# A loop over passes of two rounds, hand-written semaphores, and three larger pieces in two places

## The chip, the core and the metric

The kernel runs on one core of one Trainium2 chip. Four parts of the core matter here: VectorE (DVE in the profile), ScalarE (ACT), SyncE (SP), which issues the transfers, and the 16 DMA engines that move bytes between the on-chip buffer (SBUF, 128 partitions) and the chip's memory. The metric is the device time of one execution in microseconds, the median of several runs.

## The reference

For each of 4,096 rows of 256 numbers, all products of two numbers of the row are computed, and the upper triangle (with the diagonal) is kept: 256 x 257 / 2 = 32,896 float32 numbers per row.

```python
dot = jnp.einsum('bi,bj->bij', inputs, inputs)     # inputs: (4096, 256) float32
iu, ju = jnp.triu_indices(d)                       # d = 256
return dot[:, iu, ju]                              # (4096, 32896) float32
```

The input is 4.19 MB, the output 538.97 MB. In the output, a row is a sequence of runs: run i holds x[i] * x[i:], 256 - i numbers long.

## The kernel before

A partition holds 32 input rows. They are worked off in 16 groups of two rows (`REPEAT`). Of each group, the 32,896 output columns are cut into five pieces; each piece is computed for both rows into one of three buffers of a pool and stored with one DMA per row. The very first piece is cut further, so that stores can start early.

```python
UNIT = 64
REPEAT = 2
PIECES = 5
BUDGET = 0.95
FIRST = [512, 1536, 3584]
...
opool = ctx.enter_context(tc.tile_pool(name="o", bufs=3))
x_out = out.rearrange("(p g r) c -> g p r c", p=P, r=REPEAT)
...
cuts = [0, REPEAT * d, total // 2, total]
for a, b in zip(cuts, cuts[1:]):
    nc.sync.dma_start(xt[:, a:b], x_in[:, a:b])

for g in range(groups):
    for c, (lo, hi) in enumerate(zip(borders, borders[1:])):
        o = opool.tile([P, REPEAT, slot], F32, tag="o", name=f"o_{g}_{c}")
        first = g == c == 0
        cuts = [lo, *(FIRST if first else []), hi]
        for a, b in zip(cuts, cuts[1:]):
            block = runs(d, a, b)
            k = split(block, 0.0 if first else BUDGET * REPEAT * (b - a))
            for i, j, at, length in block[:k]:              # ScalarE: one run, one row
                for r in range(REPEAT):
                    nc.scalar.activation(o[:, r, ...], xt[...], AF.Copy, scale=xt[...])
            for (i, j, at, length), m in interleave(block[k:]):   # VectorE: one or two runs, both rows
                nc.vector.tensor_tensor(o[:, :, ...], window(xt...), window(xt...), ALU.mult)
            for r in range(REPEAT):
                nc.sync.dma_start(x_out[g][:, r, a:b], o[:, r, a - lo : b - lo])
```

`split` gives runs to ScalarE until what is left for VectorE fits in a budget (in ns, per column and row), or until ScalarE would take longer than VectorE. Its account of the two engines is in the kernel:

```python
def vector_time(block):
    return sum(68 + 1.046 * REPEAT * n * m for (*_, n), m in vector_ops(block))
...
scalar += REPEAT * (184 + 0.837 * block[k][3])
```

The 16 groups are unrolled in Python: the program has each group's instructions in full. The framework places the semaphores.

## Time and profile before

| What | Value |
|---|---|
| time, median of 3 runs | 1274.3 us (1274.18 to 1274.4) |
| span of the profiled execution | 1272.5 us |
| multiplications on VectorE | 1812, mean 634 ns |
| idle time of VectorE ahead of them | 239.9 us, of which 191.1 ended by a store that landed |
| runs on ScalarE | 1546, mean 404 ns |
| read from memory, written to it | 4.19 MB, 538.97 MB |

The page counts the busy time of each engine, shows the span in 40 slices (a digit is the busy share in tenths), the DMA queues with packets and bytes, and the chain of work that ended last. A packet is one contiguous stretch that one DMA engine moves. The times "to landing" run from the issue of a DMA on SyncE until its semaphore has been raised by all 16 engines, so they hold the time in line behind earlier DMAs too. Tables of stretches give, for each stretch of time, each engine's busy time with the number of instructions, and the mean share of the 16 DMA engines that was busy.

### The profile page before, as it was taken

To read this page: it belongs to the slowest core of one execution; us is meant where nothing else is said; L and a number is where in the kernel's file an instruction comes from. 1 tells how busy PE (TensorE), PEld (TensorE's weight loads), DVE (VectorE), ACT (ScalarE), POOL (GpSimd) and SP (SyncE) were. 2 spreads that over 40 slices of the span, in tenths; PEclk is the share of its full clock that TensorE was granted. 3 is DMA by queue.
4 is the path that set the end of the run, shared out by engine and by line. 5 is a ranking of instruction groups with operands and counts; after the bars stand their busy time and mean duration, and the time that the engine had idled before them with its cause. 6 is when DMAs were issued, how large, how long until landed. Compare 5 with 4: busy or idle time off the path is not lost.

```text
span 1272.5 us, 3975 instructions
## 1 busy us (share of the span) xinstructions
DVE 996.1 (78%) x1813; ACT 486.7 (38%) x1547; POOL 0.2 (0%) x4
## 2 busy tenths in 40 slices
DVE  8987887878777787777877777777777777777770
ACT  5523535234342433424334252342523425234250
POOL 0000000000000000000000000000000000000000
DMA  9999999999999999999999999999999999999998
GB/s 384 435 433 430 434 433 427 434 432 427 431 428 432 429 430 431 429 431 429 433 427 431 429 431 429 431 430 430 429 432 427 433 427 432 428 432 429 431 427 346
DMA packets 24367, 543.43 MB, mean 427 GB/s; under 512 B 2704, under 2 KB 2704, under 8 KB 3344
## 3 DMA queue, kind: packets, MB, share of 16 engines
q1 hardware_dynamic: 24336, 543.17, 99.8%
q14 instruction: 31, 0.25, 0.0%
HBM read 4.19 MB, written 538.97 MB: 427 GB/s over the span
## 4 chain that ended last, share of the span: by engine, by line
DMA 70%; DVE 25%; issue 1%; SPq 1%; DVEq 0%
DMA out_dram<-o 70%; DVE o L132 25%; SPq L139 1%; DMA x<-in_r_inputs_dram 1%; DVEq L132 0%; SPq L110 0%
## 5 line engine op out<-in xcount | busy, mean ns | idle before, releaser
L132 DVE TENSOR_TENSOR o<-x 128x356 f32<-128x356 f32 (+61 forms) x1812 | 996.1, 634 | 239.9 <-DMA out_dram<-o 191.1
L123 ACT ACTIVATE o<-x 128x253 f32<-128x253 f32 (+41 forms) x1546 | 485.4, 404 | 748.6 <-DMA out_dram<-o 732.8
L123 ACT ACT_TABLE_LOAD x1 | 1.3, 1283 | 0.7 <-PEq L154 0.7
L107 DVE MEMSET x<- 128x1 f32 x1 | 0.1, 59 | 0.8 <-PEq L154 0.8
L154 POOL MEMSET const-uint8-127<- 128x1 uint8 x1 | 0.1, 102 | 0.0
L154 POOL MEMSET const-bfloat16-1.0<- 128x1 bf16 x1 | 0.1, 101 | 0.0
L154 POOL MEMSET const-float32-0.0<- 128x1 f32 x1 | 0.1, 98 | 0.2 <-issue 0.2
L154 POOL MEMSET const-float32-1.0<- 128x1 f32 x1 | 0.1, 98 | 0.0
## 6 DMA issues: line engine op xcount, KB each, us to landing
out_dram<-o SPq DMA_DIRECT2D x128, 3296.0 KB, 27.2
out_dram<-o SPq DMA_DIRECT2D x30, 3264.0 KB, 28.9
out_dram<-o SPq DMA_DIRECT2D x2, 1472.0 KB, 13.3
x<-in_r_inputs_dram SPq DMA_DIRECT2D x1, 2048.0 KB, 12.3
out_dram<-o SPq DMA_DIRECT2D x2, 1024.0 KB, 10.0
x<-in_r_inputs_dram SPq DMA_DIRECT2D x1, 1792.0 KB, 6.8
out_dram<-o SPq DMA_DIRECT2D x2, 512.0 KB, 10.2
out_dram<-o SPq DMA_DIRECT2D x2, 256.0 KB, 10.0
```

Source lines behind the costliest of these rows:

```text
L107: nc.vector.memset(xt[:, total:], 0.0)
L123: nc.scalar.activation(o[:, r, at - lo : at - lo + length], xt[:, row + j : row + j + length], AF.Copy, scale=xt[:, row + i : row + i + 1],)
L132: nc.vector.tensor_tensor(o[:, :, at : at + m * length], window(xt[:, row + j :], [[d, REPEAT], [1, m], [1, length]]), window(xt[:, row + ...
L139: nc.sync.dma_start(x_out[g][:, r, a:b], o[:, r, a - lo : b - lo])
L154: nc = _bacc.Bacc("TRN2", target_bir_lowering=False, num_devices=1)
```

## The change

The same products are computed and stored, in another frame:

- Three pieces per group instead of five (44 KB per row instead of 26), so each place holds 2 x 44 KB. There are two such places instead of three buffers. The borders are multiples of 32 columns instead of 64.
- One DMA stores both rows of a piece.
- The 16 groups ("rounds") are taken two at a time: a pass has two rounds. The first pass is written out, the other seven are a loop on VectorE, ScalarE and SyncE[...]. The purpose is a program that is short and whose loop body stays where it is.
- [...] in each round VectorE and ScalarE each copy the group's two rows to buffers of their own (`xv`, `xa`), and read from these.
- Semaphores are written by hand. A wait that is passed takes its amount back from the semaphore, so that the next pass finds it at zero. VectorE counts its own instructions, and each waits until all but the one before it are done.
- The budget for VectorE is 0.9 instead of 0.95 ns.

The core of the diff (cuts marked with ...):

```diff
-UNIT = 64
+UNIT = 32
 REPEAT = 2
-PIECES = 5
-BUDGET = 0.95
+PIECES = 3
+PLACES = 2
+ROUNDS = 2
+BUDGET = 0.9
 FIRST = [512, 1536, 3584]
...
+    def take(self, engine, value: int):
+        engine.wait_ge(self.sem, value).then_inc(self.sem, -value)
...
-    opool = ctx.enter_context(tc.tile_pool(name="o", bufs=3))
+    xt = pool.tile([P, groups // ROUNDS, ROUNDS * each], F32, name="x")
+    xv = pool.tile([P, each + 1], F32, name="xv")
+    xa = pool.tile([P, each], F32, name="xa")
+    places = [pool.tile([P, REPEAT, slot], F32, name=f"o{k}") for k in range(PLACES)]
...
+        def add(self, ins, back: int = 1):
+            if self.count > back:
+                ins._wait_ge(v_own, self.count - back)
+            ins.then_inc(v_own, 1)
+            self.count += 1
...
+    def rounds(h, first: bool):
+        work = VectorWork()
+        for p in range(ROUNDS * PIECES):
+            r, c = divmod(p, PIECES)
+            k = p % PLACES
+            lo, hi = spans[c]
+            start = first and p == 0
+            if c == 0:
...
+                work.add(nc.vector.tensor_copy(xv[:, :each], x_now))
+                work.end()
+                nc.scalar.activation(xa, x_now, AF.Copy).then_inc(a_own, 1)
+                nc.scalar.wait_ge(a_own, 1).then_inc(a_own, -1)
+            if not (first and p < PLACES):
+                free[k].take(nc.vector, 16 * stores[k])
+                nc.vector.sem_inc(go.sem, 1)
+                go.take(nc.scalar, 1)
+            cuts = [lo, *(FIRST if start else []), hi]
             for a, b in zip(cuts, cuts[1:]):
                 block = runs(d, a, b)
...
+                vector_part(work, places[k], lo, block[share:])
+                work.end()
+                nc.vector.sem_inc(v_done.sem, 1)
+                if share:
+                    scalar_part(places[k], lo, block[:share])
+                    nc.scalar.wait_ge(a_own, 1).then_inc(a_own, -1)
+                nc.scalar.sem_inc(a_done.sem, 1)
+                v_done.take(nc.sync, 1)
+                a_done.take(nc.sync, 1)
+                nc.sync.dma_start(
+                    x_out[bass.ds(h, 1), r, :, :, a:b].rearrange("o p r c -> p (o r) c"),
+                    places[k][:, :, a - lo : b - lo],
+                ).then_inc(free[k].sem, 16)
...
+    rounds(0, first=True)
+    with nc.Fori(
+        1,
+        groups // ROUNDS,
+        1,
+        engines=ENGINES,
+        head_slot={mybir.EngineType.DVE: 0, mybir.EngineType.Activation: 0},
+    ) as h:
+        rounds(h, first=False)
```

## The prediction

> **What bounds the kernel now.** I read the slices and the queues of the page first, then the chain of waits, then the groups, then single stretches. The page:

> ```profile
> span 1272.5 us, 3975 instructions
> DVE 996.1 (78%) x1813; ACT 486.7 (38%) x1547; POOL 0.2 (0%) x4
> DMA  9999999999999999999999999999999999999998
> GB/s 384 435 433 430 434 433 427 434 432 427 431 428 432 429 430 431 429 431 429 433 427 431 429 431 429 431 430 430 429 432 427 433 427 432 428 432 429 431 427 346
> DMA packets 24367, 543.43 MB, mean 427 GB/s; under 512 B 2704, under 2 KB 2704, under 8 KB 3344
> q1 hardware_dynamic: 24336, 543.17, 99.8%
> q14 instruction: 31, 0.25, 0.0%
> DMA 70%; DVE 25%; issue 1%; SPq 1%; DVEq 0%
> out_dram<-o SPq DMA_DIRECT2D x128, 3296.0 KB, 27.2
> ```

> The DMA engines are full in every slice but the ends, near 430 GB/s, and VectorE is idle for 22% of the span. So the bytes bound it; the 25% of VectorE in the chain of waits only says that a free buffer is followed by 12.4 us of work. A store lands 27.2 us after issue though its own bytes take 3.375 MB / 430 GB/s = 7.85 us: over three stores stand in line, and that backlog hides VectorE. The timeline shows the same from its side:

> ```profile
> 92.68 12.42 DVE L132 TENSOR_TENSOR o<-x 128x768 f32<-128x768 f32 x17 [3.25 <-DMA out_dram<-o]
> 1208.32 12.38 DVE L132 TENSOR_TENSOR o<-x 128x612 f32<-128x612 f32 x21 [3.07 <-issue]
> 1224.10 12.74 DVE L132 TENSOR_TENSOR o<-x 128x372 f32<-128x372 f32 x48 [3.40 <-DMA out_dram<-o]
> ```

> A piece is 12.4 to 12.7 us of multiplying and then 3 to 4 us of waiting. Last, the table of stretches at both ends (us, DVE, ACT, POOL busy, PEclk, DMA share, GB/s):

> ```profile
> 0.00:10.00 10.00, 6.32 (x12) 7.88 (x19) 0.20 (x4) 1.00 0.84 336
> 10.00:20.00 10.00, 10.00 (x13) 9.19 (x27) 0.00 (x0) 1.00 0.99 370
> ...
> 1265.00:1266.00 1.00, 0.00 (x0) 0.00 (x0) 0.00 (x0) 1.00 0.50 211
> 1266.00:1267.00 1.00, 0.00 (x0) 0.00 (x0) 0.00 (x0) 1.00 0.19 79
> 1267.00:1269.00 2.00, 0.00 (x0) 0.00 (x0) 0.00 (x0) 1.00 0.18 79
> 1269.00:1270.00 1.00, 0.00 (x0) 0.00 (x0) 0.00 (x0) 1.00 0.12 53
> 1270.00:1271.00 1.00, 0.00 (x0) 0.00 (x0) 0.00 (x0) 1.00 0.06 26
> ```

> A share of 0.19 is 3 of 16 engines, 0.12 two, 0.06 one. Thirteen engines are done soon after 1266 and three stragglers run on to about 1271, the last some 5 us behind. The time is that of the slowest DMA engine.

> [...] The trace agrees: its packet records have medians of 84 ns for 2,048 B, 159 for 4,096, 309 for 8,192 and 980 for 26,368, which is about 9 ns plus 0.0368 ns per byte. [...] The trace has 31 instruction packets of 8 KB (309 ns each), so the fetches do share the DMA engines; that they sit on the three stragglers is my inference. [...]

> **The change part by part.**

> (a) Fewer packets. A store is 128 partitions x 2 rows, one packet each. Before: 80 pieces x 256 = 20,480, three extra cuts in the first piece x 256 = 768, loads 384: 21,632. After: 48 x 256 = 12,288, plus 768, plus 384: 13,440. That is 8,192 fewer. The 4-byte packets at a DMA's end fall from 169 x 16 to 54 x 16, 1,840 fewer. Per engine (8,192 + 1,840) / 16 = 627 packets x 9 ns = 5.6 us less. The bytes stay. All of it lies on the path. [...]

> (b) Fewer instruction fetches. By the built programs, VectorE goes from 1,894 instructions in the body[...] to 244 ahead of the loop and 242 in it; ScalarE from 1,705 to 242 and 223. [...] some 4 packets per engine. If one straggler carries VectorE's 15, it loses 11 x 309 ns = 3.4 us. I take 3.5[...].

> (c) The loop and its steps. Each round adds a copy of 512 elements on VectorE and one on ScalarE (by the neighbours in the groups, 0.5 to 0.7 us each), each piece a few semaphore steps (50 ns each on VectorE by the median of its semaphore instructions), each pass a branch. They stand where VectorE waits for a free place: off the path while slack is left.

> (d) Is there slack with two places? A store moves 2 x 43.9 KB x 128 = 11.24 MB, 26.1 us at 430 GB/s. A place comes free when its store has landed, and that is when the other store starts. Then: VectorE's part by the kernel's own account 19.5 to 19.7 us (the same account gives 12.26 to 12.44 for the old pieces, and the timeline 12.38 to 12.74, so I take 19.9); the start and landing of a DMA, 2.1 us (the first load, 256 KB, lands 2.7 us after issue, and its bytes take 0.6); semaphore hops and addresses, about 1. Sum 23.0, slack 3.1 us in each 26.1. ScalarE's largest part is 16.0 us and hides behind VectorE's. So the queue stays full, with 3 us instead of a backlog of nearly 20. Cost 0.

> (e) The start, where slack isn't yet built up. The first piece is cut at the same three columns, but its last part is now 7,360 columns instead of 2,944. VectorE's share of the four parts is 1.2 + 1.8 + 3.0 + 9.9 = 16.0 us. From 3.4, where the first load has landed, with 1.0 for the copy and a later entry and 0.8 for the four hand-overs, it is done at 21.2; the store flows at 22.4. The DMAs have 4.19 MB of loads and 3.67 MB of stores until then; by the table they moved 7.06 MB in 20 us, so they run dry near 22: no gap worth counting. The fourth part, 7.54 MB, lasts 17.5 us, to 40. The second piece needs VectorE from 21.3 to 41.2 and flows at 42.5. Gap 2.5 us, paid once.

> (f) Entry and exit of the hand-written part: a barrier at each end and the waits at the end, +0.8 us.

> Sum: -5.6 + 0.3 - 3.5 + 2.5 + 0.8 = -5.5. 1274.3 - 5.5 = 1268.8 us.

> **The rivals.**

> Two places starve the queue. If the hand-over costs 4 us more than I think (own-count waits on each multiplication, the branch, a slow address), slack turns into a gap of 1 us in each of 46 periods: 1320 us. For it: 3.1 us is thin, and the engines differ by 3 to 5 us in when they end. Against it: the program before has such a wait on nearly every multiplication too, and its pieces take what the kernel's account says, and an engine that runs ahead only waits for the slowest, which keeps its work in line.

> The loop fetches its body again in each pass. The line that ends in "issue" shows VectorE held up for about 3 us, and there are 15 of these; at each back edge it would fall into the 6 us in which VectorE waits anyway. The packets would stay as many as they were: (b) falls away, 1272.

> The bytes alone count. [...] (a) is worth 2 and the start eats the rest: 1273.

> VectorE as the bound: 16 x (19.5 + 19.7 + 19.7) = 942 us is far below the span. I discard it.

> **Range and chances.** The known terms go from -13[...] to +2 (no packet gain, a start gap of 4). Within them, 1264 to 1275 should hold 8 times in 10. Faster by over 2% needs 25 us[...]. Chance 0.01. Slower by over 2% needs the first rival in every period: 0.04. Within 2%: 0.95.

> **What would show it.** (a): about 14,300 packets and 432 GB/s in middle slices. (b): instruction packets near 10, and stragglers that end within 2 us of the rest. (c), (d): waits of VectorE for a store of 4 to 7 us in each period, and no slice in the middle below 9. (e): a DMA share below 1 for 2 to 3 us near 40 us. A dip in every period, or some 30 instruction packets, would prove me wrong in (d) or (b).

## The result, and the profile after

The changed kernel takes 1275.49 us (median of 4 runs, 1275.45 to 1275.53) against 1274.25 us before: a ratio of 1.001, with a 95% interval of 0.9992 to 1.0027. The prediction was 1268.8 us, with a range of 1264 to 1275.

The first part of the page of the changed kernel, its slices and queues:

```profile
span 1273.5 us, 4059 instructions
DVE 952.5 (75%) x1748; ACT 535.1 (42%) x1601; POOL 0.2 (0%) x4
DMA  9999999999999999999999999999999999999997
DMA packets 14315, 543.26 MB, mean 427 GB/s; under 512 B 864, under 2 KB 864, under 8 KB 1504
q1 hardware_dynamic: 14304, 543.17, 99.2%
q14 instruction: 11, 0.09, 0.0%
```

The packets fell from 24,367 to 14,315 and the instruction packets from 31 to 11, as predicted. The DMA engines are still full, and the rate over the whole span is 427 GB/s as before. In the middle it is hardly higher, first before, then after:

```profile
100.00:1200.00 1100.00, 873.45 (x1583) 421.76 (x1344) 0.00 (x0) 1.00 1.00 430
100.00:1200.00 1100.00, 837.90 (x1529) 463.73 (x1393) 0.00 (x0) 1.00 1.00 431
```

So the packets were saved, and the time that they had cost went elsewhere. The two ends show a part of it. Stretches of the changed kernel (us, DVE, ACT, POOL busy, PEclk, DMA share, GB/s; a packet is credited to the stretch in which it begins, and one lasts 1.6 us, so single shares are coarse):

```profile
38.00:40.00 2.00, 2.00 (x4) 0.00 (x0) 0.00 (x0) 1.00 0.55 236
40.00:42.00 2.00, 1.65 (x5) 0.73 (x3) 0.00 (x0) 1.00 0.21 88
42.00:44.00 2.00, 2.00 (x6) 2.00 (x8) 0.00 (x0) 1.00 1.41 597
1264.00:1266.00 2.00, 0.00 (x0) 0.00 (x0) 0.00 (x0) 1.00 0.81 351
1266.00:1268.00 2.00, 0.00 (x0) 0.00 (x0) 0.00 (x0) 1.00 0.06 22
1268.00:1270.00 2.00, 0.00 (x0) 0.00 (x0) 0.00 (x0) 1.00 0.10 44
1270.00:1272.00 2.00, 0.00 (x0) 0.00 (x0) 0.00 (x0) 1.00 0.00 0
```

Near 40 us the DMAs are dry: the packet records have nothing from 40.1 to 42.0. At the end one engine is left over: from 1268 on a share of 0.10 over 2 us is two packets of 1.62 us, one after the other on one engine. The trace also records each raise of a store's semaphore (a "mark" below; it doesn't say of which engine). Fifteen of the 16 engines mark the last store as done between 1267.36 and 1267.52, the sixteenth at 1271.79. The kernel waits for all 16 marks of a store (`free[k].take(nc.vector, 16 * stores[k])`, and `free[k].take(nc.sync, 16)` at the end), and the span ends 1.7 us after the last of them. So the sixteenth mark costs 4.3 us here.

In between VectorE has time to spare. The timeline of the changed kernel (start, length, instructions; in brackets the idle time before):

```profile
1193.76 19.70 DVE L158 TENSOR_TENSOR o<-xv 128x788 f32<-128x788 f32 x26 [6.54 <-DVEq L93]
1219.70 20.03 DVE L158 TENSOR_TENSOR o<-xv 128x484 f32<-128x484 f32 x62 [6.25 <-DVEq L93]
```

Where it waited 3 us for a buffer before, it waits 6 us for a place in each period of 26 us. From the last mark of a store at 1219.48 to the issue of the next store into the same place it is 20.6 us (issued at 1240.10), and the first packets begin 0.9 us later, at 1240.99. The late engine ends the store before at 1245.85, so it has 4.9 us to spare. The other 15 ended it near 1240.8 and stood still for some 0.2 us. From 770 us on the last mark stays 4.4 to 4.8 us behind the median of the 16: the slack is used up, and the others are held to the late engine's pace, since a place is free only when it, too, is done. Two places are enough for the engine that sets the time.

### The profile page after: what moved, and what is told of

The parts are those of the page before. It is cut to its first block, busy times and chain, and to the rows that moved or that the text cites. A ratio compares the mean times of both kernels' runs of the same rounds, so it can differ in the third digit from the quotient of the medians.

```text
span 1273.5 us, 4059 instructions
## 1 busy us (share of the span) xinstructions
DVE 952.5 (75%) x1748; ACT 535.1 (42%) x1601; POOL 0.2 (0%) x4
## 2 busy tenths in 40 slices
DMA packets 14315, 543.26 MB, mean 427 GB/s; under 512 B 864, under 2 KB 864, under 8 KB 1504
## 3 DMA queue, kind: packets, MB, share of 16 engines
q1 hardware_dynamic: 14304, 543.17, 99.2%
HBM read 4.19 MB, written 538.97 MB: 427 GB/s over the span
## 5 line engine op out<-in xcount | busy, mean ns | idle before, releaser
L158 DVE TENSOR_TENSOR o<-xv 128x672 f32<-128x672 f32 (+27 forms) x1731 | 945.6, 632 | 269.0 <-DVEq L93 268.4
L170 ACT ACTIVATE o<-xa 128x253 f32<-128x253 f32 (+49 forms) x1584 | 523.8, 423 | 686.5 <-ACTq L93 685.7
L193 DVE COPY xv<-x 128x512 f32 (+1 forms) x16 | 6.8, 427 | 17.3 <-issue 8.2
L195 ACT ACTIVATE xa<-x 128x512 f32 (+1 forms) x16 | 10.1, 630 | 13.4 <-issue 6.1
## 6 DMA issues: line engine op xcount, KB each, us to landing
out_dram<-o SPq DMA_DIRECT2D x1, 2048.0 KB, 12.4
```

What stands on the lines that cost most here:

```text
L158: nc.vector.tensor_tensor(o[:, :, at : at + m * length], window(xv[:, j:], [[d, REPEAT], [1, m], [1, length]]), window(xv[:, i:], [[d, REP ...
L170: ins = nc.scalar.activation(o[:, r, at - lo : at - lo + length], xa[:, r * d + j : r * d + j + length], AF.Copy, scale=xa[:, r * d + i : ...
L193: work.add(nc.vector.tensor_copy(xv[:, :each], x_now))
L195: nc.scalar.activation(xa, x_now, AF.Copy).then_inc(a_own, 1)
```

## The experiments

The order is that of the question: is it the fetches, the start, the engine itself, the bytes or the instructions? A ratio is against the kernel before, whose medians beside the experiments are 1274.20 to 1274.28 us.

**The loop written out** (e1).

```diff
-    with nc.Fori(1, groups // ROUNDS, 1, engines=ENGINES, head_slot=...) as h:
+    for h in range(1, groups // ROUNDS):
         rounds(h, first=False)
```

Expected:

> The changed kernel with its eight passes written out instead of looped; all else stays. Theory A (instruction fetches make the DMA engines that end last): about 30 instruction packets come back, one engine ends some 3 us later, and the time is 1278 to 1279 us. Rival B (the engine that ends last is slow for another reason, such as what it does to the stores themselves): the packets come back too, the time stays within 1 us of 1275.5.

Measured: 1275.08 us, ratio 1.0007 (0.9999 to 1.0015). Its queue row and its tail:

```profile
q14 instruction: 30, 0.25, 0.0%
```

```profile
1266.00:1268.00 2.00, 0.00 (x0) 0.00 (x0) 0.00 (x0) 1.00 0.16 66
1268.00:1270.00 2.00, 0.00 (x0) 0.00 (x0) 0.00 (x0) 1.00 0.15 66
1270.00:1272.00 2.00, 0.00 (x0) 0.00 (x0) 0.00 (x0) 1.00 0.05 22
```

The fetches came back, 30 instead of 11, and the time did not rise. There are more late engines (the last three marks are 1.3, 4.1 and 4.5 us behind the median), but the last is hardly later: 4.5 us for 4.4. What is gained lies behind it: from the last mark to the end of the span it is 1.2 us, with the loop 1.7. Theory A falls, and with it the reason for the loop: it saves nothing that can be seen.

Fetches can still have cost something on the way. In the changed kernel eight of the 11 instruction packets fall between 126 and 234 us (309 to 400 ns each, 2.6 us in all), and meanwhile the last mark goes from 0.7 to 3.4 us behind the median. After that none falls until the work is over, and the marks show two engines: one falls back, to 1.6 us at 667 us; another rises, from 1.6 us at 302 us to 4.5 at 770 us, while some 650 multiplications and 590 ScalarE instructions run. The delay that lasts grows without fetches.

**The second piece's first store cut in two** (e2).

```diff
+SECOND = [13696]
-            cuts = [lo, *(FIRST if start else []), hi]
+            cuts = [lo, *(FIRST if start else SECOND if first and p == 1 else []), hi]
```

> The changed kernel with the store of the second piece of the first pass cut in two (2,752 and 8,224 columns), so that the DMAs have work when the first piece's last part is done. Theory A (the dry stretch of 1.9 us near 40 us is a loss that is never given back): no dry stretch, 1273.5 us. Rival B (the time is set by how fast places come free later on, and the start is made up there): 1275.5 us.

Measured: 1273.54 us, ratio 0.9995 (0.9987 to 1.0003). The same stretches as above:

```profile
38.00:40.00 2.00, 2.00 (x4) 0.00 (x0) 0.00 (x0) 1.00 0.77 327
40.00:42.00 2.00, 1.24 (x4) 0.65 (x3) 0.00 (x0) 1.00 0.96 407
42.00:44.00 2.00, 2.00 (x5) 2.00 (x7) 0.00 (x0) 1.00 0.94 391
```

The share at 40 us goes from 0.21 to 0.96 and the time falls by 1.95 us, the length of the gap (1.87 us). Here the dry start is paid in full.

**Stores alone, in both shapes** (e3, e4). All computing is left out; zeros are stored.

```diff
-    (products, and waits between the engines)
+    for k in range(PLACES):
+        nc.vector.memset(places[k], 0.0).then_inc(filled, 1)
...
+            if n_store >= PLACES:
+                free[k].take(nc.sync, 16 * 1)
+            nc.sync.dma_start(x_out[...], places[k][...]).then_inc(free[k].sem, 16)
```

> Stores alone: no products are computed, two places of zeros are stored over and over with the changed kernel's shape, 48 DMAs of 2 x 44 KB per partition, two in line; the loads stay. Per packet overhead of 5 ns (the pitch of the last engine's packets): the stores take 1253 us of DMA time on each engine, 3 us less than in the next run. Overhead of 9 ns, as predicted: 5.6 us less. If instruction fetches make the stragglers, all 16 engines end within 1 us here; if one engine is slow by itself, it ends 3 to 5 us after the rest.

> Stores alone in the shape of the kernel before: 160 DMAs of one row of 26 KB per partition, three places of two DMAs in line; no products are computed. 3 us longer than the run with the 44 KB shape if a packet costs 5 ns, 5.6 us if 9 ns, under 1 us if the packet's size doesn't matter. Stragglers as in that run.

Measured: 1300.05 us with 44 KB, 1301.38 us with 26 KB. The fills ahead of the first store differ, so I count from its issue (47.45 and 42.93 in the timelines): 1252.60 against 1258.45 us. The larger packets save 5.85 us, which is 9.4 ns for each of the 624 packets that an engine moves less (13,056 and 23,040 of them on 16 engines). And in both runs all engines end together, within 0.4 and 0.7 us by the marks. The end with 44 KB:

```profile
1294.00:1296.00 2.00, 0.00 (x0) 0.00 (x0) 1.00 0.81 351
1296.00:1298.00 2.00, 0.00 (x0) 0.00 (x0) 1.00 0.00 0
```

In these two runs no engine is slow by itself.

**The same bytes in few instructions, and few bytes in the same instructions** (e5, e9).

```diff
 # e5: runs of a piece -> one or two stretches; a run of 128 products repeats
-        for (i, j, at, length), m in interleave(block):
+        for at, m, length in stretches(block):
...
-                    window(xv[:, j:], [[d, REPEAT], [1, m], [1, length]]),
+                    window(xv[:, 0:], [[d, REPEAT], [0, m], [1, length]]),
 # e9: all instructions, at most 16 columns each
+            length = min(length, SHORT)
```

> The changed kernel with the same places, stores and waits, and the same number of elements written on each engine, but in few long instructions: each piece's runs are replaced by one or two stretches in which a run of 128 products repeats, so the products are not the right ones (loop body 38 instructions on VectorE and 51 on ScalarE instead of 242 and 223). Theory C (the number of small instructions delays one or more DMA engines): all 16 engines end within 1 us, and the time is 4 us shorter, about 1271. Rival D (the bytes that VectorE and ScalarE write to the buffer and read from it disturb the DMAs' reading): the last engine still ends 4 us late, 1275.

> The other way round: the changed kernel with all its instructions and waits, but each multiplication writes at most 16 columns per run and row; the rest of a place holds zeros from the start (two fills of a place, about 35 us, stand ahead of the first store, so the whole is some 25 to 30 us longer for that alone). Theory C (number of instructions): one or more engines still end 4 us after the rest. Rival D (bytes in the buffer): all end within 1 us.

Measured: e5 takes 1265.95 us, ratio 0.9935 (0.992 to 0.995), 9.5 us less than the changed kernel. Its tail:

```profile
1258.00:1260.00 2.00, 0.00 (x0) 0.00 (x0) 0.00 (x0) 1.00 1.53 659
1260.00:1262.00 2.00, 0.00 (x0) 0.00 (x0) 0.00 (x0) 1.00 0.11 44
1262.00:1264.00 2.00, 0.00 (x0) 0.00 (x0) 0.00 (x0) 1.00 0.00 0
```

All engines end within 0.9 us. VectorE's parts are shorter here (834.3 us busy in all for 952.5), so the second store is issued at 38.4 instead of 41.1 and the start isn't dry; that is 1.95 of the 9.5 us. The other 7.6 us go with the short instructions. About half of it shows at the end (the last mark 0.7 us behind the median, not 4.4). Most of the rest is lost on the way, as the others are held to the late engine's pace: from the second store to the last, a store takes 26.00 us by the median marks in e5 and 26.06 in the changed kernel, 3.1 us over 46 stores. In e9 (1308.98 us, with 35 us of fills ahead) the bytes are gone, the instructions are there, and so is the late engine:

```profile
1298.00:1300.00 2.00, 0.00 (x0) 0.00 (x0) 0.00 (x0) 1.00 0.10 44
1300.00:1302.00 2.00, 0.00 (x0) 0.00 (x0) 0.00 (x0) 1.00 0.05 22
1302.00:1304.00 2.00, 0.00 (x0) 0.00 (x0) 0.00 (x0) 1.00 0.05 22
```

By its marks the last store ends on 15 engines by 1299.34 and on the sixteenth at 1305.26. Both runs say the same: it is the number of instructions; the bytes that they write are not needed for it. Fetches can't stand in for it: e5 has fewer (5), but e9 has the changed kernel's 11 and is later.

**Slack** (e6), `BUDGET = 0.9` to `0.82`:

> The changed kernel with VectorE's budget at 0.82 instead of 0.9, so that ScalarE takes more and VectorE's parts are 17.9, 17.9 and 18.6 us instead of 19.5, 19.7 and 19.7: 1.1 to 1.8 us more slack between a free place and the next store. If the waits of the fast DMA engines for the slow one cost time: 1 to 2 us shorter, 1274. If the slow engine alone sets the end and is never without work: unchanged, or a little longer since there are some 10% more instructions on ScalarE.

Measured: 1274.23 us, 1.26 us less, the number of the first expectation. But the second store is issued 1.7 us earlier (39.41 instead of 41.10), and the dry start shrinks from 1.9 to 0.2 us:

```profile
39.00:40.00 1.00, 0.20 (x2) 0.00 (x0) 0.00 (x0) 1.00 0.01 0
40.00:41.00 1.00, 0.26 (x1) 0.22 (x1) 0.00 (x0) 1.00 1.65 702
```

That is more than the gain; after the start it is 0.4 us longer. At the end the last engine's mark is 5.4 us after the fifteenth instead of 4.3. So the waits of the other engines for it cost nothing, as the second expectation says: with less slack it is only less far behind, since the others are held up for it.

**The pieces alone, in the kernel before** (e8).

```diff
-UNIT = 64, PIECES = 5, BUDGET = 0.95, bufs=3
+UNIT = 32, PIECES = 3, BUDGET = 0.9, bufs=2
```

> The kernel before (unrolled, the framework's semaphores, one DMA per row) with the pieces alone changed: three pieces, two buffers, borders at multiples of 32, budget 0.9. If the pieces give the gain of the packets and the loss of the dry start, and the loop with its own semaphores gives nothing: the same as the changed kernel within 1 us, 1274.5 to 1276. If the hand-written waits or the copies cost something: 2 us or more below it.

Measured: 1274.01 us, ratio 0.9999 (0.9991 to 1.0008): 1.5 us less than the changed kernel. That lies between the two expectations. Its dry start is 0.7 us instead of 1.9, and it has no entry and exit of a hand-written part. The loop, the copies and the own semaphores bring nothing over it.

```profile
39.00:40.00 1.00, 0.65 (x3) 0.00 (x0) 0.00 (x0) 1.00 0.01 0
40.00:41.00 1.00, 0.47 (x1) 0.44 (x2) 0.00 (x0) 1.00 1.67 702
```

**Few instructions on one engine at a time, and in the kernel before** (e10, e11, e13). The edit is that of e5, on VectorE alone, on ScalarE alone, and in the kernel before on both.

> The changed kernel with few long instructions on VectorE alone (the products repeat and are not the right ones); ScalarE keeps its 1,584 short ones. If the delay of the last DMA engine goes by all instructions alike: about half of it, the last engine 3 to 4 us after the rest, 1269 to 1270 us. If it comes from VectorE's instructions, each of which raises a semaphore and waits for one: gone, 1266. If it comes from ScalarE's: all of it, 6 to 7 us, 1273.

> The mirror image: few long instructions on ScalarE, VectorE keeps its 1,731 products with their waits. All instructions alike: last engine 3 to 4 us late and, with the dry start of 1.9 us, 1271 to 1272. VectorE's instructions alone: 1275. ScalarE's alone: 1268.

> The kernel before (five pieces, three buffers, one DMA per row) with few long instructions on both engines; the products repeat and are not the right ones. If the count of instructions delays the last engine here too: all 16 end within 1 us, 1269 us. Against the changed kernel with few instructions (1265.95 us) the difference is then the packets' alone, less a start that is no longer dry: 4 to 5.6 us, 1270 to 1271.5. If the number of instructions doesn't matter in this kernel: 1274.

Measured: 1267.26, 1272.59 and 1269.67 us. With few instructions on both engines it was 1265.95. Counted up from there, ScalarE's 1,384 more instructions cost 1.3 us (0.95 ns each), and VectorE's 1,630 more cost 6.6 us, of which 1.95 are the dry start, so 4.7 us or 2.9 ns each. Counted down from the changed kernel it is more: 2.9 us for ScalarE's (2.1 ns each) and 8.2 less 1.95 for VectorE's (3.9 ns each). The two don't add up to the 9.5 us of both together, so each has a range. Neither expectation of equal shares nor of one engine alone held: it is mostly VectorE's. In the kernel before, the short instructions cost 1274.25 - 1269.67 = 4.6 us (its last mark is then 1.3 us behind the median instead of 5.3).

**A larger budget** (e12), the cut of e2 and `BUDGET = 1.0`:

> A version meant to be faster, with the right products: the second piece's store cut in two as before, and a budget of 1.0, which moves runs from ScalarE (two instructions for each run) to VectorE (one for both rows): 1,060 instead of 1,584 on ScalarE, about 1,860 instead of 1,731 on VectorE, 12% fewer in all. VectorE's part grows to 21.9 us of a period of 26.1, slack about 2 us. By the count of instructions: 0.9 us less than the 1273.54 of the cut alone, 1272.6. If 2 us of slack is too little: 1275 or more.

Measured: 1273.35 us, ratio 0.9993 (0.9985 to 1.0002), 0.2 us less than the cut alone. The estimate took all instructions as equal. With the shares just found, 504 fewer on ScalarE are worth 0.5 to 1.1 us and 142 more on VectorE take 0.4 to 0.6 back: little is left, as measured.

**Raises of the semaphore** (e14, e15, e16).

```diff
 # e14, e15 (with the cut of e2): runs taken from six parts in turn, a raise on about every third
-            work.add(
...
+            ins = nc.vector.tensor_tensor(
...
+            if n in raises:
+                work.add(ins)
 # e16: ScalarE raises on each instruction
-        ins.then_inc(a_own, 1)
+                ins.then_inc(a_own, 1)
```

> The changed kernel with the right products, but VectorE raises its own semaphore on about one multiplication in three instead of on each: a piece's runs are taken from six parts in turn, so that an instruction has to wait only for the one six before it (about 82 raises per pass instead of 216; some 10% more instructions on VectorE). If the raises delay the last DMA engine: its delay falls from 7.4 us to 3 or so, and the time by 3 to 4 us, to 1271.5 to 1272.5. If VectorE's instructions as such do it: unchanged or up to 0.7 us longer, 1275.5 to 1276.2.

> The same with the store of the second piece of the first pass cut in two, which took 1.95 us off the changed kernel. If the raises are the cause: 1269.5 to 1270.5, below both kernels. If they are not: 1273.5 to 1274.

> The changed kernel, in which each of ScalarE's 1,584 instructions also raises ScalarE's own semaphore, instead of the last one of each part; nothing waits more often. If raises delay a DMA engine: one or more end later by 4 us or more than in the changed kernel, 1278 to 1280 (less, about 1276, if ScalarE's raises fall on another engine than VectorE's and that one is not the last). If VectorE's instructions as such are the cause: 1275.5.

Measured: 1276.60, 1273.73 and 1277.42 us. e16 adds 1.93 us for 1,533 more raises (ScalarE's last instruction of each part raised before, too), 1.3 ns each. e14 seems to speak against it: 1,073 raises fewer, and 1.1 us longer. But its start is worse. More and shorter instructions in the first parts let the second store land 1.97 us later than in the changed kernel (medians of the marks, 70.45 and 68.48), and 225 more instructions are run. After the start it gains 0.9 us, and so does e15 against e2 (0.2 us longer in all, its second store lands 1.1 us later). At the rates found below, 1,073 raises are worth 1.3 us and 225 multiplications cost 0.5. That raises alone are the cause fell; that they are a part of it stands.

**Short instructions beside stores alone** (e18, e19): 1,728 multiplications on VectorE, 16 columns each, into a buffer that isn't stored.

```diff
+    with nc.Fori(0, 54, 1, engines=OrderedEngineSet([mybir.EngineType.DVE]), ...):
+        for n in range(32):
+            ins = nc.vector.tensor_tensor(short[:, n], ..., ALU.mult)
+            ins.then_inc(v_short, 1)          # e18: each; e19: the last of 32
```

> Stores alone as in the run with the 44 KB shape (1300.05 us, all engines end together), and beside them, in the first 210 us, 1,728 short multiplications on VectorE into a small buffer that is not stored, each of which raises a semaphore. If VectorE's instructions as such and their raises delay a DMA engine: the last ends 5 us late or more, 1305 to 1307. If raises alone: 2 us, 1302. If only instructions that write what is stored: 1300.

> The same with a raise only after every 32nd multiplication. If VectorE's instructions as such do it: 3 to 5 us late, 1303 to 1305, some 2 us less than with the raises. If raises do it: as without any multiplications, 1300. If the two runs are alike and late, raises count for nothing here.

Measured: 1303.72 and 1301.65 us, against 1300.05 with stores alone. The multiplications of e18 and its end:

```profile
L156 DVE TENSOR_TENSOR xa<-xv 128x16 f32<-128x16 f32 x1728 | 152.1, 165 | 21.8 <-DVEq L163 21.8
1296.00:1298.00 2.00, 0.00 (x0) 0.00 (x0) 1.00 0.05 22
1298.00:1300.00 2.00, 0.00 (x0) 0.00 (x0) 1.00 0.05 22
```

How far the last of the 16 marks of a store lies behind the median of the 16:

| store that lands near | stores alone | with multiplications (e19) | with a raise each (e18) |
|---|---|---|---|
| 75 us | 0.1 us | 0.5 us | 0.8 us |
| 153 us | 0.2 us | 2.4 us | 3.5 us |
| 231 us (all multiplications done) | 0.1 us | 3.8 us | 5.8 us |
| 517 us | 0.2 us | 2.9 us | 4.9 us |
| the last, 1297 us | 0.2 us | 1.6 us | 3.9 us |

The delay of one engine grows while the multiplications run (47 to 222 us), by 3.7 us over 1,728 or 2.1 ns each, and by 3.3 ns each with a raise. Then it stops growing and shrinks by some 2 us in 1,060 us. This is the delay by itself: no instruction packet falls between 12 and 965 us, and the multiplications share no place with the stores and wait for none. How a multiplication holds up the engine is not shown.

**A version with what the runs showed** (e17): the kernel before with the three pieces of e8, one DMA for both rows, and the cut of e2.

```diff
-                for r in range(REPEAT):
-                    nc.sync.dma_start(x_out[g][:, r, a:b], o[:, r, a - lo : b - lo])
+                nc.sync.dma_start(x_out[g][:, :, a:b], o[:, :, a - lo : b - lo])
```

> A version with the right products: the kernel before, unrolled and with the framework's semaphores, with three pieces in two buffers, one DMA for both rows, and the second piece's first store cut in two. Against the same without the cut and with a DMA per row (1274.0 us): no dry start, 0.7 to 1.5 us less, and 52 DMAs less, 0.3 us: 1272.3 to 1273. If the exit and entry of the hand-written part cost nothing, it equals the changed kernel with the cut, 1273.5.

Measured: 1270.94 us, ratio 0.9974 (0.9964 to 0.9983), under both kernels and under the expectation. Its end:

```profile
1262.00:1264.00 2.00, 0.00 (x0) 0.00 (x0) 0.00 (x0) 1.00 0.16 66
1264.00:1266.00 2.00, 0.00 (x0) 0.00 (x0) 0.00 (x0) 1.00 0.15 66
1266.00:1268.00 2.00, 0.00 (x0) 0.00 (x0) 0.00 (x0) 1.00 0.05 22
```

Of the 3.1 us under e8, the dry start is 0.7, and 0.3 was expected of the saved DMAs. Some 2 us are left. Here two engines are equally late (marks at 1268.1 and 1268.3), in e8 the last stands alone (1269.4 and 1271.3), and it lies 5.3 us behind the median against 4.8 here; that this is where the 2 us went is not shown. Why the delay falls on one engine in one program and on two or three in another was not found. What the traces do show: the four programs that are written out, with 28 to 31 instruction packets, all end with two or three late engines; most looped ones, with 11 to 13, end with one.

## Why the prediction was wrong

(a) Fewer packets: right in mechanism and size for stores alone, -5.85 us against -5.6. Between the two kernels with few instructions (e5, e13) it is less: -3.7 us, or -4.8 when the entry and exit of (f) are taken off. The 1.0 us between isn't explained. The 0.3 us that the sum adds back was a guess, and no run tests it.

(b) Fewer instruction fetches, -3.5 us: wrong, and this is the step that failed. The count was right (11 packets, from 31). The inference that "one straggler carries VectorE's 15", and that its loss would be saved, was not: the trace does not say whose instructions a packet holds or which DMA engine moves it, so the 15 and the one straggler were my guess. With the fetches back the time is 0.4 us shorter (e1), and the stragglers that were to end within 2 us of the rest end 4.4 us behind. What makes the last engine late is the number of short instructions (e5, e9, e18, e19). That number the change hardly touched (1,748 + 1,601 busy instructions, from 1,813 + 1,547), so nothing could be gained there.

What the prediction had no term for at all: the delay grew. The short instructions cost 4.6 us before (e13) and 1275.49 - 1265.95 - 1.95 = 7.6 us after (e5, the dry start taken off). The rates fit the 7.6: 1,731 multiplications with a raise at 3.3 ns are 5.7 us, and ScalarE's 1,584 at 0.95 to 2.1 ns are 1.5 to 3.3, so 7.2 to 9.0 us. They don't fit the 4.6: VectorE's 1,812 multiplications and some 1,700 raises of its semaphore, with ScalarE's 1,546 instructions, would give 7.4 us or more there too. So why the same instructions cost 3.0 us less in the kernel before stays open. There three engines are late, by 3.4 to 5.3 us, and in the changed kernel one; but the changed kernel written out (e1) has three late ones and takes about as long.

(c) The copies and semaphore steps: 0, as far as can be seen. They lie in VectorE's 6 us of waiting; no run takes them out alone, and what their raises add to the late engine's delay was not measured.

(d) Two places: the cost of 0 was right, but the queue stays full only on the late engine, which has 4.9 us left where 3.1 was worked out, with 1 us in it that was guessed for semaphores and addresses. From 770 us on the other 15 have no slack, since the late engine has used it up. It costs nothing, as they would only wait at the end instead, and more slack (e6) brings nothing but an earlier second store.

(e) The dry start: right, 1.95 us against 2.5.

(f) Entry and exit: right. The first load is issued at 0.97 instead of 0.73 us, and from the last mark to the end of the span it is 1.7 us instead of 0.9: 1.1 us against the 0.8 that was guessed.

The sum of what was measured: between the two kernels with few instructions, -3.7 us (packets, entry and exit together); the dry start, +1.95; the delay of the last engine, +7.6 - 4.6. That is +1.2 us, and 1275.49 - 1274.25 = 1.24. The sum closes by its making: e5, e13 and the two kernels are both sides of it. What it shows is where the 6.7 us between -5.5 and +1.24 lie: 3.5 that (b) promised and did not bring, and 3.0 by which the delay grew.

Of the rivals, the refetching loop did not come about, and the starved queue only as the 0.2 us in which 15 engines wait for the last. The third came nearest in time (1273), and for the wrong reason: the packets do count (5.85 us, e3 against e4).

## What to carry to other kernels

The span ends 0.9 us after the last mark of a store in the kernel before, 1.2 us in e1 and 1.7 us in the changed kernel, with all DMA engines full until the last few us: the time is the last engine's. So where they are full, look at the shares in the last few us before looking at rates, and when some engine is late, try the same bytes with few instructions (here e5, 9.5 us shorter) before blaming what happens to share its name. That fetches and late engines stand in the same trace is no cause; one run with the loop written out told. Larger pieces saved 5.85 us by their packets with stores alone, and in the changed kernel the large second piece cost 1.95 us, since nothing was left to store near 40 us; its first store cut in two (e2) saves that.

## What the runs showed of the hardware

A fetch of 8 KB (a packet of 309 ns) goes with a delay, too: with 44 KB stores alone (e3) the only one falls at 965 us; the last mark goes from 0.3 to 0.75 us behind the median, and is back at 0.3 within 110 us.
